# Folding some of the A f products into the A (E - 1) g sums of a graph-attention kernel

## The chip, the cores and the metric

The kernel runs on one core of a Trainium2 chip. The metric is the device time of one execution in microseconds. The engines are named as the profile names them: PE (matrix multiply; PEld is its weight load), DVE (vector), ACT (scalar), POOL and SP, which here mostly issue DMAs.

## The reference

Layer 0 is graph attention over 4096 nodes with a dense 0/1 adjacency A, 8 heads of 64 features; layer 1 is attention inside 32 graphs of 128 nodes. Each is followed by a residual and a layer norm.

```python
feats = jnp.einsum('nf,hfo->hno', X, W)
s_self = jnp.einsum('hno,ho->hn', feats, a_self)
s_neigh = jnp.einsum('hno,ho->hn', feats, a_neigh)
dense = s_self[:, :, None] + s_neigh[:, None, :]
dense = jnp.where(dense > 0, dense, ALPHA * dense)
dense = dense * A[None, :, :]
attn = jax.nn.softmax(dense, axis=-1)
out = jnp.einsum('hij,hjo->hio', attn, feats) + b[:, None, :]
...
a = jnp.where(mask, query @ key.T * scale, 0.0)
scores = (a + b + edge_encoding) * jnp.where(mask, 1.0, -1000000.0)
softmax = jax.nn.softmax(scores, axis=-1) * mask
return softmax @ value
```

Pairs without an edge have the score 0, and so the weight exp(0) = 1. The numerator of layer 0 is therefore the sum of all features, plus the sum over edges of (E - 1) f, where E is the exponential of the score. E is a product of a row factor, a column factor and the larger of two terms, p of the row and d of the column; that is how it is made from two vectors without an exponential for each pair. In the code g is f scaled by its column factor, and u is the row factor that the sum A f still lacks.

## The kernel before

After a setup that makes the features and the exponentials, four passes (`main_pass`, r = 0 to 3) treat two heads each. A pass goes through four chunks c of C = 1024 rows, and a chunk through NT = 32 steps j of 128 neighbours. For a step:

- DVE makes q[j, h] = max(p_row, d_j) * A for both heads (L1475, 128x1024);
- a mark per pair of q is made for the denominators, on ACT (L1485), except for the second head of every fourth step (j % 4 == 3), which DVE makes (L1480);
- PE adds -A f in four matmuls of 128x128 weights to the PSUM tile `accf` (L1499), and A E g in eight matmuls of 32 columns to the tile `acc` (L1521), four of which run beside each other in the array;
- PE adds marks to `dens` (L1536), for eight steps at a time.

At the end of a chunk, `sums_to_rows` makes y = (accf + S) * u + acc on DVE (L1259, L1267), and its pieces, run later, turn y by PE (L1339), divide it (L1340 into `hst`) and send it to memory, or in the last pass hand it to layer 1.

PE's instructions are in the order of the program. Those of the other engines are ordered by a scheduler when the kernel is built, and each engine then works through its queue in that order.

Passes 0 to 2 take groups of eight steps (`wide=8`): all accf matmuls of the group, then all of acc, then dens. Pass 3 takes groups of four. The q tiles go round in a ring of 8 buffers in the wide passes and 6 in the last; a buffer is free when the acc matmuls of its step are done. In pass 0 the adjacency is turned by PE and cast by ACT (L610, L621) and written out; the later passes read it back (`bring`).

In pass 3, from chunk 1 on, `run_plan` puts pieces of layer 1 between the groups by the table PLAN: `pieces(c, group, 0)` between accf and acc, `pieces(c, group, 1)` after dens. "E" is the end of the chunk before; "a" and "b" are the two blocks of 512 rows of that chunk, nine pieces each (`layer_1`: L1075 turns x1, L1095 makes z, L1122 the scores, L1167 the values, L1181 the output); "F" ends a layer norm and "R" starts the second block. `rows_of_layer_0` adds the residual and takes the statistics (L1246, L512). Small PSUM tiles (`misc`, ps_m) go round three banks from pass 1 on. `load_block` and `check_block` stream the adjacency once more to see that it holds only 0 and 1, two ACT operations a block (L1230, L1231).

```python
PLAN = [("E", "b"), ("b", "Fb"), ("b", "a"), ("Ra", "a"), ("Fa", "b"), ("ba", "b")]
PLANS = PLAN + [("ab", ""), ("aaba", "")], PLAN + [("a", ""), ("aa", "a")]
```

Of the kernel before, what the change touches and what calls it, by code (L numbers as in the profile page):

```python
# [10 lines left out]
F32 = mybir.dt.float32  # L11
# [8 lines left out]
P = 128  # L20
# [384 lines left out]
def adjacency_streamed_path(  # L405
# [57 lines left out]
    f_d = dram.tile([PR, NT // 4, P, 4 * 2 * FP], F32, name="f_d")  # L463
    pu_d = dram.tile([2 * H, N], F32, name="pu_d")
    at_d = dram.tile([NCH, NT, P, C], F32, name="at_d")
# [28 lines left out]
    n0 = const.tile([P, NT], F32, name="n0")  # L494
    nb_all = const.tile([P, NT, H], F32, name="nb_all")
    e_all = early.tile([P, NT, 2, H], F32, name="e_all")
    e_b = const.tile([P, NT, H, 6], BF16, name="e_b")
# [39 lines left out]
    hp_ = ctx.enter_context(tc.tile_pool(name="hout", bufs=1))  # L537
    ckp = ctx.enter_context(tc.tile_pool(name="ck", bufs=2))
    ps0 = ctx.enter_context(tc.tile_pool(name="ps_misc", bufs=1, space=PSUM))
# [92 lines left out]
    with tc.tile_pool(name="setup1", bufs=1, side="right") as one, tc.tile_pool(  # L632
# [97 lines left out]
        def exponentials(k, u, sc):  # L730

            j = 4 * k + u
            if u == 0:
                pu_js[k] = two.tile([P, 4, 2, H], F32, name="pu_j")
# [9 lines left out]
            nc.scalar.activation(pu_js[k][:, u], st[:, 3:5], AF.Exp)  # L744
            nc.scalar.activation(d_all[:, j, :], st[:, 2], AF.Exp)

        def parts_of_exponentials(k):
            blk = slice(4 * k, 4 * k + 4)
            nc.vector.tensor_scalar_mul(
                nb_all[:, blk, :], d_all[:, blk, :], -BIG * (1.0 + 2.0**-23)  # L750
            )
            eb = e_b[:, blk]
            for i in range(2):
# [11 lines left out]
        def rows_of_exponentials(k):  # L765
            pr = pss.tile([2 * H, 4, P], F32, name="ps_set")
            for u in range(4):
                nc.tensor.transpose(
                    pr[:, u, :], pu_js[k][:, u].rearrange("p k h -> p (k h)"), ident
                )  # L770
            if k < NB - 1:
                row = late.tile([2 * H, 4 * P], F32, name="pu_row")
            else:
                row = hp_.tile([P, CT, FP], F32, name="hst")
                row = row.rearrange("p t n -> p (t n)")[: 2 * H, : 4 * P]
            rows[k] = row
# [6 lines left out]
        def columns_of_exponentials(k, pc=None):  # L783
            pc = pss.tile([P, 4, 2 * H], F32, name="ps_set") if pc is None else pc
            for u in range(4):
                nc.tensor.transpose(pc[:, u, :], rows[k][:, ts(u, P)], ident[: 2 * H, : 2 * H])
            nc.vector.tensor_copy(
# [140 lines left out]
    def columns_of_last():  # L928

        columns_of_exponentials(NB - 1, misc([P, 4, 2 * H]))  # L930

    psa = ctx.enter_context(tc.tile_pool(name="ps_acc_f", bufs=1, space=PSUM))
    dens = psa.tile([P, HB], F32, name="dens")
# [135 lines left out]
    def layer_1(blk, x1b, lp, lp1, lp2):  # L1069
# [47 lines left out]
        pq = misc([P, 4, P])  # L1117
        ns = lp1.tile([P, 4, P], F32, name="ns")
        nm = small.tile([P, 4], F32, name="nm_f")
# [130 lines left out]
    def sums_to_rows(r, c, acc, accf, ae, u_row, later_by):  # L1250
# [25 lines left out]
        def pieces():  # L1276
# [127 lines left out]
    def main_pass(r, ae=None, wide=4):  # L1404

        for c in range(NCH):
# [8 lines left out]
            for h in range(2):  # L1415
# [5 lines left out]
                    ),  # L1421
                )
            def pieces(c, group, place):
                if r == PR - 1 and c:
# [21 lines left out]
            for j0 in range(0, NT, wide):  # L1446
# [14 lines left out]
                if at_step == 0:  # L1461
                    cast_steps(0, 6, last_pair)
                follow = [
                    x
# [4 lines left out]
                for j in cycle:  # L1469
                    for h in range(2):  # L1470
                        hh = 2 * r + h
                        q = qs[j, h] = ring("q", qp, 6).tile([P, C], F32, name="q")
                        d_j = d_all[:, j, hh : hh + 1]
                        with following(at_step == 0, ("DVE", 3 if j else 2)):
                            ends_of_setup["Q"] = nc.vector.scalar_tensor_tensor(  # L1475
# [40 lines left out]

                for j in cycle:
                    for s in range(2):
                        for o in range(0, FP, 32):
                            h = o // FH  # L1520
                            nc.tensor.matmul(  # L1521
                                acc[o : o + 32, s, :],
                                g_s[j // 4][:, j % 4, h, o % FH : o % FH + 32],
                                qs[j, h][:, ts(s, HB)],
                                start=(j == 0),
                                stop=(j == NT - 1),
                            )
                if r == 0:
# [118 lines left out]
```

## Time and profile before

| what | us |
|---|---|
| median of three runs (2055.07 to 2056.7) | 2055.48 |
| the profiled execution, its own time | 2057.91 |
| its span, first to last instruction | 2056.1 |
| a chunk of pass 0, from L1259 to L1259 | 106.2 |
| a chunk of pass 1 or 2 | 93 to 106 |
| the chunks 0 to 3 of pass 3 | 104.9, 140.7, 170.5, 163.6 |

The end of chunk c of pass 3 is where L1259 starts, at 1443.5, 1584.3, 1754.7 and 1918.3; pass 0 ends so at 565.4. The granted TensorE clock is 0.994 over the span. In the profile a line of a group has the instruction, its output and inputs, the count, then the busy time of all, the mean of one in ns, and the idle time of the engine before them with what ended it. Matmuls overlap, so their mean is longer than their share of the busy time, and one that waits for its input can still count as busy.

### The profile page before, as it was taken

The numbers are of one execution on the slowest core, as the hardware profiler recorded it, in microseconds if no ns is written. First come the engines' busy times: TensorE is split into PE (matmuls) and PEld (weight loads), VectorE is DVE, ScalarE is ACT, GpSimd is POOL, SyncE is SP. The second block draws the span as 40 slices with busy tenths as digits, with TensorE's granted clock in tenths as the row PEclk, the third lists the DMA queues.
The fourth block names the chain that finished last, engine by engine and source line by source line (L and its number), as shares of the span: only waits on it lengthen the run. The fifth ranks groups of instructions, "written<-read, shape, count | busy, mean of one in ns | idle before, by whom it ended". The sixth has DMA issues, their size and how long they took to land.

```text
span 2056.1 us, 38302 instructions
## 1 busy us (share of the span) xinstructions
PE 2030.4 (99%) x15105; PEld 1051.0 (51%) x15105; DVE 1671.9 (81%) x2125; ACT 1542.2 (75%) x1878; POOL 224.2 (11%) x361
## 2 busy tenths in 40 slices
PE   9999999999999999999999999999999999999997
PEld 7884555555544444444454444544454445545453
DVE  5668888888899998798998999999975984896654
ACT  3349888888879889788898989998885666567420
POOL 1222222222100000000000000000210210210111
PEclk9999999999999999999999999999999999999999
DMA  6999999999999999798999999989974764775211
GB/s 208 245 325 259 287 288 276 291 268 289 271 373 337 354 352 335 257 310 298 319 323 340 316 336 323 326 295 358 323 237 144 250 242 137 225 274 169 73 49 43
DMA packets 207371, 551.31 MB, mean 268 GB/s; under 512 B 24780, under 2 KB 65740, under 8 KB 207180
## 3 DMA queue, kind: packets, MB, share of 16 engines
q1 hardware_dynamic: 142828, 426.31, 59.6%
q0 software_dynamic: 62272, 121.91, 23.2%
q8 instruction: 121, 1.98, 0.4%
q10 hardware_dynamic: 2080, 0.52, 0.1%
q14 instruction: 70, 0.57, 0.1%
HBM read 491.79 MB, written 107.22 MB: 291 GB/s over the span
## 4 chain that ended last, share of the span: by engine, by line
PE 93%; DVE 4%; issue 1%; DMA 1%; SPq 0%; POOL 0%; ACT 0%; POOLq 0%; DVEq 0%
PE acc L1521 41%; PE accf L1499 23%; PE ps_fe L800 5%; PE ps_m L1167 5%; PE dens L1536 5%; PE ps_m L1095 5%; DVE q L1475 3%; PE ps_m L1122 1%; PE ps_m L610 1%; PE ps_m L1181 1%; PE ps_m L1075 1%; PE ps_m L1024 1%; PE ps_m L1339 1%; PE ps_set L720 1%; PE ae L1435 1%
## 5 line engine op out<-in xcount | busy, mean ns | idle before, releaser
L1475 DVE SCALAR_TENSOR_TENSOR q<-p_row,d_all,at 128x1024 f32<-128x1024 f32 x1024 | 1242.0, 1277 | 146.9 <-PE acc L1521 121.1
L1485 ACT ACTIVATE mark<-q,nb_all 128x1024 fp8e4<-128x1024 f32 x896 | 995.5, 1145 | 184.3 <-DVE q L1475 168.6
L1521 PE MATMUL acc<-q,g_s 128*32 128x512 f32 x8192 | 903.4, 593 | 1.1 <-DVE q L1475 0.4
L1521 PEld LDWEIGHTS acc<-q,g_s 128*32 128x32 f32 x8192 | 264.1, 110 | 594.4 <-issue 533.0
L1499 PE MATMUL accf<-at,f_s 128*128 128x512 f32 x2048 | 495.2, 398 | 2.1 <-ACT at L621 2.1
L1499 PEld LDWEIGHTS accf<-at,f_s 128*128 128x128 f32 x2048 | 380.3, 188 | 110.4 <-issue 26.4
L1230 ACT ACTIVATE ck<-ck,neg_half_f 128x1024 f32<-128x1024 f32 x128 | 146.0, 1141 | 25.5 <-DMA ck<-in_adj_dram 25.4
L1231 ACT ACTIVATE ck<-ck,neg_quarter 128x1024 f32<-128x1024 f32 x128 | 146.3, 1143 | 1.7
L1536 PE MATMUL dens<-mark,e_b 128*6 128x512 fp8e4 x2048 | 125.3, 379 | 0.0
L800 PE MATMUL ps_fe<-w_sb_f,xT_f 128*128 128x264 f32 (+1 forms) x512 | 121.1, 393 | 1.9 <-ACT xT_f L723 1.9
L621 ACT CAST at<-ps_m 128x1024 fp32r<-128x1024 fp8e4 x124 | 116.4, 1025 | 4.8 <-PE ps_m L610 4.3
L1167 PE MATMUL ps_m<-wvT,x1T 128*128 128x512 f32 x256 | 114.2, 594 | 0.0
L1095 PE MATMUL ps_m<-x1T,M_sb 128*128 128x512 f32 x256 | 112.9, 594 | 0.0
L800 PEld LDWEIGHTS ps_fe<-w_sb_f,xT_f 128*128 128x128 f32 x512 | 100.1, 199 | 16.4 <-ACT xT_f L723 2.5
L1350 POOL DMA_DIRECT2D hs_d<-hst x12 | 10.7, 896 | 847.8 <-DVE hst L1340 847.8
L1480 DVE TENSOR_SCALAR mark<-q,d_all 128x1024 fp8e4<-128x1024 f32 x128 | 96.3, 752 | 4.7
L622 POOL DMA_DIRECT2D at_d<-at x128 | 69.0, 541 | 272.3 <-ACT at L621 248.1
L1536 PEld LDWEIGHTS <-e_b 128*6 128x6 bf16 x2048 | 54.7, 86 | 77.7 <-issue 34.6
L1095 PEld LDWEIGHTS ps_m<-x1T,M_sb 128*128 128x128 f32 x256 | 48.0, 190 | 59.3 <-issue 58.4
L1167 PEld LDWEIGHTS ps_m<-wvT,x1T 128*128 128x128 f32 x256 | 47.6, 190 | 56.4 <-issue 55.2
L1175 DVE TENSOR_TENSOR v_t<-ps_m,bv_row 128x512 f32<-128x512 f32 x32 | 21.7, 684 | 60.5 <-PE ps_m L1167 60.5
L1102 ACT ACTIVATE zT<-ps_m,zb 128x512 f32<-128x512 f32 x32 | 21.7, 680 | 61.2 <-PE ps_m L1095 61.2
(195 smaller groups left out, 1099.5 us busy)
## 6 DMA issues: line engine op xcount, KB each, us to landing
at<-at_d SPq DMA_DIRECT2D x384, 512.0 KB, 6.3
f_s<-f_d SPq DMA_DIRECT2D x128, 512.0 KB, 7.8
at_d<-at POOLq DMA_DIRECT2D x128, 512.0 KB, 14.8
ck<-in_adj_dram SPq DMA_DIRECT2D x128, 512.0 KB, 5.5
g_s<-g_d SPq DMA_DIRECT2D x128, 256.0 KB, 5.6
f_d<-fst POOLq DMA_DIRECT2D x16, 1024.0 KB, 7.9
a_b<-in_adj_dram POOLq DMA_DIRECT2D x32, 512.0 KB, 17.4
p_row<-pu_d SPq DMA_DIRECT2D x32, 512.0 KB, 6.9
```

The costliest lines, as they stand in the source:

```text
L621: ends_of_setup["ACT"] = nc.scalar.copy(at, both[:, :, k])
L800: nc.tensor.matmul(pf[:, q, :, cols], tile_j(xTs[k][:, c].rearrange("p u n -> p (u n)"), u), w_sb[:, c, 4 * q : 4 * q + 4, cols], start=(c ...
L1095: nc.tensor.matmul(pz, L1["M"][:, f, ts(c, P)], x1T[:, f, :], start=(f == 0), stop=(f == FC - 1),)
L1167: nc.tensor.matmul(pv, x1T[:, f, ts(u, P)], L1["wvT"][:, f, :], start=(f == 0), stop=(f == FC - 1),)
L1230: tc.keep_in_program_order(nc.scalar.activation(ck, ck, AF.Square, bias=neg_half))
L1231: nc.scalar.activation(ck, ck, AF.Abs, bias=neg_quarter, accum_out=binp[:, k : k + 1])
L1475: ends_of_setup["Q"] = nc.vector.scalar_tensor_tensor(q, p_row[h], d_j, ats[r, c, j].bitcast(F32), op0=OP.max, op1=OP.mult)
L1480: nc.vector.tensor_scalar(mark, q, d_j, None, op0=OP.is_gt, saturate=False)
L1485: nc.scalar.activation(mark, q, AF.Sigmoid, bias=nb_all[:, j, hh : hh + 1], scale=BIG, saturate=False,)
L1499: nc.tensor.matmul(accf[:, s, :], f_s[j // 4][:, j % 4, w, :], ats[r, c, j][:, ts(s, HB)], start=(j == 0 and w == 0), stop=(j == NT - 1 an ...
L1521: nc.tensor.matmul(acc[o : o + 32, s, :], g_s[j // 4][:, j % 4, h, o % FH : o % FH + 32], qs[j, h][:, ts(s, HB)], start=(j == 0), stop=(j ...
L1536: nc.tensor.matmul(dens[lo : lo + 6, :], e_b[:, j, 2 * r + h, :], marks[j, h][:, ts(s, HB)], start=(j == 0), stop=(j == NT - 1),)
```

## The change

For some steps, called folded, the four A f matmuls are left out. DVE makes q in two operations instead: max(p_row, d_j) times a row U that holds 1/u, then minus a column c = 1/e, times A. With g as the weights this is (E - 1) f over the row factor u, so the eight matmuls of the step add it to `accf`, not to `acc`, and L1259 multiplies it by u later. The mark is a sigmoid of q against a constant.

Folded are, in pass 3, the steps j % 4 == 2 below 28 of chunks 1 to 3 (seven in each); in pass 0, the steps j % 8 == 6 below 24 (6, 14 and 22; in chunk 0 only 14 and 22).

The rows U are loaded once a chunk: in pass 0 into the two `ck` tiles, in pass 3 into the `hst` tile and a new one of the pool lp1. Room is made for these: `ns` and `pT_f` of layer 1 become the tile `a4`, worked on in place, and pass 3 writes the divided rows over y in place of `hst`. The setup takes reciprocals for c (two a block of 512 rows) and for U (two a block, and 20 in place of 16 rows of pu_d).

```diff
+    FOLDED = (0, PR - 1)
+    HU = 2 * len(FOLDED)
+    pu_d = dram.tile([2 * H + HU, N], F32, name="pu_d")
...
+            for r in FOLDED:
+                nc.vector.reciprocal(
+                    c_all[r][:, blk], e_all[:, blk, 1, 2 * r : 2 * r + 2]
+                )
...
+            for i, r in enumerate(FOLDED):
+                nc.vector.reciprocal(
+                    pu_js[k][:, :, 2 * H + 2 * i : 2 * H + 2 * i + 2],
+                    pu_js[k][:, :, H + 2 * r : H + 2 * r + 2],
+                )
...
-        ns = lp1.tile([P, 4, P], F32, name="ns")
+        ns = a4
...
-        pT = lp1.tile([P, 4, P], F32, name="pT_f")
+        pT = a4
...
-            hst = hp_.tile([P, CT, FP], F32, name="hst")
+            if r == PR - 1:
+                hst = y.rearrange("p (t n) -> p t n", t=CT)
+            else:
+                hst = hp_.tile([P, CT, FP], F32, name="hst")
...
+            def folded(j):
+
+                if r == PR - 1:
+                    return r in FOLDED and c > 0 and j % 4 == 2 and j < NT - 4
+                return r in FOLDED and j % 8 == 6 and (0 if c else 8) < j < NT - 8
+
+            def rows_for_folded():
+
+                for h in range(2):
+                    if r == PR - 1:
+                        pool, shape, name = ((hp_, [P, CT, FP], "hst"), (pools.get("lp1"), [P, C], "U_row"))[h]
+                    else:
+                        pool, shape, name = ckp, [P, CK], "ck"
+                    row = pool.tile(shape, F32, name=name)
+                    U_row.append(row.rearrange("p t n -> p (t n)") if len(shape) == 3 else row)
+                    nc.sync.dma_start(
+                        U_row[h],
+                        broadcast_rows(pu_d[2 * H + 2 * FOLDED.index(r) + h, ts(c, C)], P, C),
+                    )
...
+                        if folded(j):
+                            cn = c_all[r][:, j, h : h + 1]
+                            nc.vector.scalar_tensor_tensor(
+                                q, p_row[h], d_j, U_row[h], op0=OP.max, op1=OP.mult
+                            )
+                            nc.vector.scalar_tensor_tensor(
+                                q, q, cn, ats[r, c, j].bitcast(F32), op0=OP.subtract, op1=OP.mult
+                            )
+                            mark = marks[j, h] = sgp.tile([P, C], FP8, name="mark")
+                            nc.scalar.activation(
+                                mark, q, AF.Sigmoid, bias=below_0, scale=2.0**80, saturate=False
+                            )
+                            continue
...
-                    for w in range(2):
+                    for w in range(0 if folded(j) else 2):
...
+                    dst = accf if folded(j) else acc
...
-                                acc[o : o + 32, s, :],
+                                dst[o : o + 32, s, :],
```

More of the change, by code (lines that the diff above doesn't have):

```diff
@@ L463, in adjacency_streamed_path @@
     f_d = dram.tile([PR, NT // 4, P, 4 * 2 * FP], F32, name="f_d")
-    pu_d = dram.tile([2 * H, N], F32, name="pu_d")
+    FOLDED = (0, PR - 1)
+    HU = 2 * len(FOLDED)
+    pu_d = dram.tile([2 * H + HU, N], F32, name="pu_d")
     at_d = dram.tile([NCH, NT, P, C], F32, name="at_d")
@@ L495, in adjacency_streamed_path @@
     nb_all = const.tile([P, NT, H], F32, name="nb_all")
+    c_all = {
+        r: (const if r else early).tile([P, NT, 2], F32, name="c_all") for r in FOLDED
+    }
+    below_0 = const.tile([P, 1], F32, name="below_0")
+    nc.gpsimd.memset(below_0, -128.0)
     e_all = early.tile([P, NT, 2, H], F32, name="e_all")
@@ L537, in adjacency_streamed_path @@
     hp_ = ctx.enter_context(tc.tile_pool(name="hout", bufs=1))
-    ckp = ctx.enter_context(tc.tile_pool(name="ck", bufs=2))
     ps0 = ctx.enter_context(tc.tile_pool(name="ps_misc", bufs=1, space=PSUM))
@@ L733, in exponentials @@
             if u == 0:
-                pu_js[k] = two.tile([P, 4, 2, H], F32, name="pu_j")
+                pu_js[k] = two.tile([P, 4, 2 * H + HU], F32, name="pu_j")
             st = small.tile([P, 5, H], F32, name="st")
@@ L743, in exponentials @@
             nc.scalar.activation(e_all[:, j], st[:, 0:2], AF.Exp)
-            nc.scalar.activation(pu_js[k][:, u], st[:, 3:5], AF.Exp)
+            nc.scalar.activation(
+                pu_js[k][:, u, : 2 * H].rearrange("p (k h) -> p k h", k=2), st[:, 3:5], AF.Exp
+            )
             nc.scalar.activation(d_all[:, j, :], st[:, 2], AF.Exp)
@@ L765, in rows_of_exponentials @@
         def rows_of_exponentials(k):
-            pr = pss.tile([2 * H, 4, P], F32, name="ps_set")
+            for i, r in enumerate(FOLDED):
[3 more added lines that the diff above has]
+                )
+            pr = pss.tile([2 * H + HU, 4, P], F32, name="ps_set")
             for u in range(4):
-                nc.tensor.transpose(
-                    pr[:, u, :], pu_js[k][:, u].rearrange("p k h -> p (k h)"), ident
-                )
+                nc.tensor.transpose(pr[:, u, :], pu_js[k][:, u], ident)
             if k < NB - 1:
-                row = late.tile([2 * H, 4 * P], F32, name="pu_row")
+                row = late.tile([2 * H + HU, 4 * P], F32, name="pu_row")
             else:
                 row = hp_.tile([P, CT, FP], F32, name="hst")
-                row = row.rearrange("p t n -> p (t n)")[: 2 * H, : 4 * P]
+                row = row.rearrange("p t n -> p (t n)")[: 2 * H + HU, : 4 * P]
             rows[k] = row
@@ L785, in columns_of_exponentials @@
             for u in range(4):
-                nc.tensor.transpose(pc[:, u, :], rows[k][:, ts(u, P)], ident[: 2 * H, : 2 * H])
+                nc.tensor.transpose(
+                    pc[:, u, :], rows[k][: 2 * H, ts(u, P)], ident[: 2 * H, : 2 * H]
+                )
             nc.vector.tensor_copy(
@@ L930, in columns_of_last @@
         columns_of_exponentials(NB - 1, misc([P, 4, 2 * H]))
+    ckp = ctx.enter_context(tc.tile_pool(name="ck", bufs=2))
     psa = ctx.enter_context(tc.tile_pool(name="ps_acc_f", bufs=1, space=PSUM))
@@ L1422, in main_pass @@
                 )
+            U_row = []
+            def folded(j):
[14 more added lines that the diff above has]
+                    )
             def pieces(c, group, place):
@@ L1462, in main_pass @@
                     cast_steps(0, 6, last_pair)
+                if not U_row and any(folded(j) for j in cycle):
+                    rows_for_folded()
                 follow = [
@@ L1473, in main_pass @@
                         d_j = d_all[:, j, hh : hh + 1]
+                        if folded(j):
[5 more added lines that the diff above has]
+                                q, q, cn, ats[r, c, j].bitcast(F32), op0=OP.subtract, op1=OP.mult
+                            )
+                            mark = marks[j, h] = sgp.tile([P, C], FP8, name="mark")
+                            nc.scalar.activation(
+                                mark, q, AF.Sigmoid, bias=below_0, scale=2.0**80, saturate=False
+                            )
+                            continue
                         with following(at_step == 0, ("DVE", 3 if j else 2)):
@@ L1526, in main_pass @@
                                 stop=(j == NT - 1),
+                                skip_group_check=folded(j),
                             )
```

## The prediction, made before the changed kernel ran

> **What bounds the kernel now.** I read the page's busy times first, then its costliest groups, then the table by stretches, then the timelines of PE and DVE inside one group of steps. The page and its groups:
>
> ```profile
> PE 2030.4 (99%) x15105; PEld 1051.0 (51%) x15105; DVE 1671.9 (81%) x2125; ACT 1542.2 (75%) x1878; POOL 224.2 (11%) x361
> ...
> L1475 DVE SCALAR_TENSOR_TENSOR q<-p_row,d_all,at 128x1024 f32<-128x1024 f32 x1024 | 1242.0, 1277 | 146.9 <-PE acc L1521 121.1
> ...
> L1521 PE MATMUL acc<-q,g_s 128*32 128x512 f32 x8192 | 903.4, 593 | 1.1 <-DVE q L1475 0.4
> ...
> L1499 PE MATMUL accf<-at,f_s 128*128 128x512 f32 x2048 | 495.2, 398 | 2.1 <-ACT at L621 2.1
> ```
>
> PE is the longest queue, and DVE is second at 81%, all its idle time spent waiting for PE to give q buffers back. That average hides two different stages. By stretches (start:end, length, then busy time of each engine; the first lies in the first pass, the second and third are the first and the second half of chunk 1 of the last pass):
>
> ```profile
> 248.00:353.00 105.00, 104.66 (x966) 52.83 (x959) 87.12 (x91) 91.58 (x90) 25.78 (x41) 1.00 1.11 285
> ...
> 1444.00:1503.00 59.00, 58.57 (x472) 27.24 (x468) 58.77 (x82) 49.77 (x70) 14.29 (x8) 1.00 0.95 322
> 1503.00:1584.00 81.00, 81.00 (x445) 40.84 (x438) 46.73 (x63) 55.91 (x77) 5.89 (x10) 1.00 0.51 167
> ```
>
> The third number is DVE: 87 of 105 in the first pass, but 58.8 of 59 where the changed steps of chunk 1 begin. Now one group of eight steps of the first pass, DVE and then PE (start, length, instruction, count, idle before):
>
> ```profile
> 381.52 10.85 DVE L1475 SCALAR_TENSOR_TENSOR q<-p_row,d_all,at 128x1024 f32<-128x1024 f32 x9 [3.80 <-PE acc L1521]
> 392.30 0.74 DVE L1480 TENSOR_SCALAR mark<-q,d_all 128x1024 fp8e4<-128x1024 f32 x1
> ```
>
> ```profile
> 378.50 1.07 PE L610 MATMUL ps_m<-ident_b,a_b 128*128 128x128 bf16 x16
> 379.49 13.94 PE L1521 MATMUL acc<-q,g_s 128*32 128x512 f32 x128
> 393.37 0.66 PE L1282 MATMUL ps_m<-ident_f,hst 128*128 128x128 f32 x4
> ```
>
> PE takes (393.37-379.49)/8 = 1.735 us for a step of acc. DVE sits full at eight q tiles (four steps), starts the fifth step's q 2.03 us after acc began, when the first step's buffers are free, and makes one q each (10.85-1.28)/8 = 1.196 us, 2.39 us for a step. The eighth q ends at 381.52+7x1.196+1.28 = 391.17; PE wants it at 379.49+7x1.735 = 391.63. So DVE, idle 3.8 us before the group, catches the last step by 0.46 us. The last pass, chunk 1, PE:
>
> ```profile
> 1450.82 3.93 PE L1499 MATMUL accf<-at,f_s 128*128 128x512 f32 x16
> 1454.59 0.60 PE L1316 MATMUL ps_m<-ident_f,dcs 128*128 128x128 f32 x4
> ...
> 1455.99 7.52 PE L1521 MATMUL acc<-q,g_s 128*32 128x512 f32 x64
> ...
> 1467.31 9.44 PE L1521 MATMUL acc<-q,g_s 128*32 128x512 f32 x62
> ...
> 1482.69 7.07 PE L1521 MATMUL acc<-q,g_s 128*32 128x512 f32 x64
> ...
> 1495.25 7.07 PE L1521 MATMUL acc<-q,g_s 128*32 128x512 f32 x64
> ```
>
> An undisturbed acc of four steps is 7.07; those of 7.52 and 9.44 waited for q inside, though PE counts as busy. DVE is what ends here. The accf group gives (1454.59-1450.82)/16 = 0.236 us a matmul.
>
> **What the Trainium skill says.** "Perfetto Trace Analysis", Identifying the Most-Contended Engine, says that busy share of matmuls misleads because they are pipelined, and its Optimization Strategy says that the contended engine can change between regimes; both hold here (the acc of 9.44 us). "TensorE: Matmul & The Clock Gate", Part 3, says that matmuls run as a strict FIFO in start and end: one late q holds all behind it. "VectorE: DVE Perf Modes", the perf-mode tier table, gives two-tensor fp32 work only the 1x rate (2293 ns for 2048 elements, so an estimate of 1.15 us for 1024); the trace has 1.196 from start to start. So no cheaper form of the added operation is to be hoped for.
>
> **The change part by part.** Folded steps: last pass 7 in each of chunks 1 to 3, 21; first pass 2 in chunk 0 and 3 in each other, 11; in all 32.
>
> Removed: 4 accf matmuls a step, 4x0.236 = 0.94 us, 32x0.94 = 30.1 us of PE. The eight matmuls of E only change their bank: 0.
>
> Added: two DVE operations a step. The second reads q, a column and the adjacency, the form of L1475, so 2x1.196 = 2.39 us a step, 76.5 us in all. They are issued h0, h1, h0, h1, so the dependent one finds its input ready. The mark stays on ACT with the same shape (1145 ns): 0.
>
> First pass. The folded step is the seventh of eight, so its extra 2.39 falls where DVE is catching up. The last q comes at 391.17+2.39 = 393.56, PE is there at 391.63: 1.93 late. From such a late q to PE's next group the trace of chunk 2 of the last pass has 1.90 us (q ends 1616.70, next 1618.60), 0.17 over a step, so 2.10. Against it 0.94 from accf: +1.16 a group. DVE's idle 3.8 before the next acc covers its own lateness, so nothing carries over. 11 x 1.16 = **+12.8**. Both ends: the wait can't fall under 1.93-0.94 = 1.0 a group, nor pass 2.39+0.17-0.94 = 1.6: +11 to +18.
>
> Last pass, chunk 1. Here the fold is the third of four steps and six q are made ahead, but DVE has no idle time to make them in. Until the fourth group's last q, DVE gets 4x2.39 = 9.6 more, and the built program's queue order puts about 3.0 us of layer-norm work (an hp_l add of 0.5; five x1b adds and two stats, 1495.03 to 1497.50) behind that q: 1499.97+9.6-3.0 = 1506.6, acc ends 1.9 later at 1508.5 against 1502.14. PE's accf savings up to there are eaten by this wait. Walking queue by queue gives 5.9. From group 4 on PE has layer-1 matmuls and DVE idles (46.7 of 81), so three folds save 0.94 each: +5.9-2.8 = **+3.1**.
>
> Chunks 2 and 3 have the same start, with less DVE load at group 0 (-0.2 there). In group 1 the queue order puts the second evacuation of the turned sums (L1340, 1621.62 before) behind the layer-norm statistics, at about 1626.1. The three banks ps_m go round, so the second values matmul (1622.57 before) waits for that bank, its v_t and the q behind it come later: +4.3 by the end of group 1. Group 2 -0.5, group 3 +3.8 (DVE bound again), groups 4 to 6 -2.8: **+4.7** each, +9.4. Both ends for the last pass: if DVE's lateness were absorbed, -0.94x21 = -19.7; if each added operation landed whole, 21x(2.39-0.94) = +30.5.
>
> Other edits. Two hp_l adds go out of chunk 0, where DVE is busy 96 of 104: -0.9. At the end of setup two reciprocals come ahead of the last row transposes, and a cast that accf waits for (L621, 156.73) goes behind the row copy: +1.0; 0 to +1.5. The other reciprocals (some 30, under 0.25 us each by L1332's row) fall in DVE's idle setup time: 0. Fourteen row loads of 512 KB (6.9 us as p_row's) are queued on SP one group ahead: 0; if SP were held behind their DVE wait, the at loads (6.3 us) behind them would be late, at most a few us for each of 3 chunks. The in-place a4, and y for hst: a buffer's reuse that the plan leaves free for groups: 0, up to +2 in the tail.
>
> Sum: 12.8 + 3.1 + 9.4 - 0.9 + 1.0 = +25.4. The profiled execution took 2057.9 with a span of 2056.1, so its span would be 2081.5; the median of the runs, 2055.48, becomes **2081**, +1.2%.
>
> **The rivals.** (a) The last pass absorbs it: DVE idles 3 to 10 us at a time in the second half of each chunk, and if late q are made up there PE keeps its 19.7: 2055.5+12.8+1.0-19.7 = 2050, faster. It decides if the acc of groups 0 to 3 grow by less in all than 0.94 a fold, some 20 us over three chunks. Against it: PE's lost time is not returned, as PE is itself full afterwards. (b) All is hidden: DVE at 81% has room on average: 2055.5-30 = 2025; against it the 0.46 us of room above. (c) Each added operation lands whole: 2055.5+76.5-30.1 = 2102; for it, DVE's 58.8 of 59 and bank waits like that of group 1 elsewhere; against it, groups 4 to 6. (d) The first pass as computed, the last one about even: 2055.5+13.8 = 2069, on the forecast's side.
>
> **How the numbers follow.** Forecast with its size errors, 2072 to 2094: 0.66; (d) 0.12; (c) 0.11; (a) 0.08; (b) 0.03. The range 2064 to 2096 takes (d), the forecast and the lower edge of (c). A measurement here tells about 0.2% (4 us) from no change. Faster: (a)+(b) with a bit less, 0.10; same 0.02; slower 0.88.
>
> **What would show it.** Right: in the first pass the acc runs of folded groups last about 16.0 in place of 13.94, and those of the fourth group of each chunk stay; accf groups of 28 matmuls; chunks of 109.7 in place of 106.2. In the last pass, acc runs of groups 0 to 3 well over 7.07, those of 4 to 6 at 7.07; DVE idle only in the second halves; chunk 1 longer by 3, chunks 2 and 3 by 5. Wrong: first-pass acc runs still of 13.94 (the ring ran further ahead than I read), or last-pass chunks shorter by 6.6, which is (a).

## The result, and the profile after

| | before | after |
|---|---|---|
| median of six runs each, us | 2055.28 (2051.77 to 2056.70) | 2080.06 (2076.24 to 2086.44) |
| ratio after/before, 95% interval | | 1.0125 [1.0108, 1.0143] |
| the profiled execution, its span, us | 2056.1 | 2080.0 |

The change costs 24.8 us, within 1 us of the forecast. The page of the changed kernel, engines and then the groups that the change touches (the numbers behind the bar: busy us, mean ns of one | idle before it, released by):

```profile
PE 2035.5 (98%) x14977; PEld 1027.0 (49%) x14977; DVE 1747.2 (84%) x2221; ACT 1535.9 (74%) x1876; POOL 235.4 (11%) x362
...
L1533 DVE SCALAR_TENSOR_TENSOR q<-p_row,d_all,at 128x1024 f32<-128x1024 f32 x960 | 1166.6, 1277 | 114.4 <-PE acc L1580 103.7
...
L1580 PE MATMUL acc<-q,g_s 128*32 128x512 f32 x7680 | 872.2, 594 | 4.4 <-DVE q L1533 1.8
...
L1557 PE MATMUL accf<-at,f_s 128*128 128x512 f32 x1920 | 468.3, 399 | 1.7 <-ACT at L627 1.6
...
L1580 PE MATMUL accf<-q,g_s 128*32 128x512 f32 x512 | 80.8, 611 | 12.3 <-DVE q L1524 9.6
L1524 DVE SCALAR_TENSOR_TENSOR q<-q,c_all,at 128x1024 f32<-128x1024 f32 x64 | 79.2, 1276 | 0.0
```

The kernel does what it says: 128 accf matmuls fewer than the 2048 of before, and 64 second operations (L1524), each as long as an L1533. PE has less to do and its busy time still rises by 5 us. The rise is the first pass's (with the folds of that pass alone PE is busy 2040.3, with those of the last pass alone 2022.7). There a folded step starts when the first head's q is there, two matmuls at a time in place of four (395.26 and 395.72 in the group shown below), and goes on when the second head's q is: that stretch counts as busy. Only the row of folded products (accf<-q) shows some of the wait in the open, 12.3 us idle. Its mean of 611 against 594 ns comes mostly from 16 matmuls of chunk 1 of the last pass that ran at half clock, of which more below.

The same stretches as before, shifted to where the chunks now lie (start:end, length, then PE, PEld, DVE, ACT and POOL; behind them PE's clock, DMA share and GB/s):

```profile
252.00:357.00 105.00, 104.03 (x926) 48.48 (x919) 93.62 (x96) 86.24 (x86) 25.39 (x41) 1.00 1.11 290
1455.00:1520.00 65.00, 58.71 (x477) 25.24 (x468) 65.00 (x81) 50.98 (x70) 28.79 (x6) 0.95 0.91 304
1520.00:1599.00 79.00, 78.86 (x419) 38.43 (x416) 57.78 (x80) 54.23 (x68) 6.76 (x9) 1.00 0.57 187
```

In the first half of chunk 1 of the last pass DVE is busy 65.00 of 65, and that half grew from 59 to 65. PE's granted clock there is 0.95, where it was 1.00 before. The second half shrank from 81 to 79, with DVE still idle for 21 us of it. So the loss lies in the first halves, and in the first pass.

For all kernels of this study I use one measure: the time from the start of one chunk's first operation of y (L1259 before, L1277 after) to that of the next, from the trace. Differences from before, us; "first" is the span's start to the first y, setup and chunk 0 together, "end" what follows the last y:

| kernel | first | pass 0, chunks 1, 2, 3 | pass 3, chunk 0 | chunks 1, 2, 3 | end |
|---|---|---|---|---|---|
| after | +2.5 | +3.36, +3.31, +3.39 | -1.6 | +3.90, +4.75, +3.39 | +0.8 |
| first pass only | +4.5 | +3.36, +3.30, +3.38 | -1.2 | +0.03, 0.00, +0.34 | -1.2 |
| last pass only | -2.3 | +0.05, -0.02, +0.03 | -0.1 | +4.19, +3.69, +2.67 | -1.6 |
| third of eight | -3.1 | -2.35, +2.43, -0.09 | +0.6 | +3.50, +3.05, +3.06 | -1.5 |
| two operations, accf kept | +5.7 | +5.83, +5.75, +5.80 | +0.5 | +0.04, -0.01, +0.39 | -1.6 |
| one operation, rows loaded | +14.7 | -2.35, -2.47, -2.38 | +0.1 | +0.05, +0.02, 0.00 | -1.3 |
| one operation, no rows | +0.1 | -2.35, -2.46, -2.38 | -1.7 | +0.03, 0.00, +0.02 | -1.6 |
| evacuations first | +1.3 | +3.37, +3.29, +3.39 | -0.8 | +3.33, +3.09, +3.04 | +1.6 |
| early half, one operation | -2.1 | +0.06, -0.02, +0.03 | -0.4 | -1.44, -1.55, -2.99 | +0.6 |
| late nine | -0.4 | +0.06, -0.04, +0.03 | +0.4 | -2.69, -2.71, -2.68 | +0.1 |
| late five a chunk | -0.1 | +0.06, -0.02, +0.03 | -1.0 | -4.52, -4.56, -4.56 | 0.0 |
| late eight a chunk | +1.5 | +0.05, -0.03, +0.02 | -0.6 | 0.00, -0.91, -1.83 | -3.8 |
| late eight and third | -1.6 | -2.38, +1.10, +1.95 | -0.2 | +0.01, -0.86, -1.74 | -3.2 |

Passes 1 and 2 never differ by more than 0.5 in a chunk. The columns "first", "chunk 0" and "end" scatter by 2 to 3 us between kernels that differ nowhere near them: the kernels without folds in the first pass have -2.3 to +1.5 in "first". PE's clock seems to have a part in it: its mean over that stretch is 0.99 in last pass only (-2.3), 0.98 before and 0.97 in late eight (+1.5). The other six columns repeat to a tenth where the code there is the same, except that in the last pass a chunk with the same folds differs by up to 1.7 us from kernel to kernel (chunk 2: +4.75 in after, +3.05 in third of eight). In the two late-eight rows the first operation of y at the end of chunk 1 stands behind other work in DVE's queue: PE starts the last acc group of that chunk 1.9 us sooner after the chunk's beginning than before, and 1.9 us of their "end" belongs to the chunks. The execution of before that the table is taken from took 2057.9, which is 2 to 3.5 us above the medians of before in the experiments: by about so much the medians show more loss, or less gain, than the chunks.

**The first pass, seen.** One folded group of eight, PE, then DVE (start, length, count, idle before):

```profile
376.91 6.97 PE L1557 MATMUL accf<-at,f_s 128*128 128x512 f32 x28
...
384.72 10.51 PE L1580 MATMUL acc<-q,g_s 128*32 128x512 f32 x96
395.26 2.68 PE L1580 MATMUL accf<-q,g_s 128*32 128x512 f32 x14
...
398.11 2.65 PE L1580 MATMUL acc<-q,g_s 128*32 128x512 f32 x14
400.69 0.66 PE L1300 MATMUL ps_m<-ident_f,hst 128*128 128x128 f32 x4
```

```profile
386.75 4.87 DVE L1533 SCALAR_TENSOR_TENSOR q<-p_row,d_all,at 128x1024 f32<-128x1024 f32 x4 [3.17 <-PE acc L1580]
391.54 2.48 DVE L1521 SCALAR_TENSOR_TENSOR q<-p_row,d_all,ck 128x1024 f32<-128x1024 f32 x2
393.93 2.48 DVE L1524 SCALAR_TENSOR_TENSOR q<-q,c_all,at 128x1024 f32<-128x1024 f32 x2
396.32 3.67 DVE L1533 SCALAR_TENSOR_TENSOR q<-p_row,d_all,at 128x1024 f32<-128x1024 f32 x3
```

From 384.72 to 400.69 the group takes 15.97; before it took 393.37-379.49 = 13.88. The first six steps (96 matmuls) run at full pace. DVE gets its first free buffer 2.03 us after acc began, as before, makes four q and the two folded ones, and ends the second L1524 at 396.41; until then PE has only the first head's half of the seventh step. The seventh and eighth step then follow DVE, not PE. DVE still has 3.17 us idle before the group, so the next group starts clean.

**The last pass, seen.** Chunk 1, group 1, PE:

```profile
1476.83 3.64 PE L1580 MATMUL acc<-q,g_s 128*32 128x512 f32 x32
1485.02 1.92 PE L1580 MATMUL accf<-q,g_s 128*32 128x512 f32 x4 [4.56 <-DVE q L1524]
1488.68 2.77 PE L1580 MATMUL accf<-q,g_s 128*32 128x512 f32 x10 [1.73 <-DVE q L1524]
...
1492.83 0.60 PE L1596 MATMUL dens<-mark,e_b 128*6 128x512 fp8e4 x4
```

This acc took 16.0 us from its start to dens; an undisturbed one takes 7. DVE in that time (it has no gap there):

```profile
1478.01 1.19 DVE L1521 SCALAR_TENSOR_TENSOR q<-p_row,d_all,hst 128x1024 f32<-128x1024 f32 x1
1479.12 1.28 DVE L1361 TENSOR_TENSOR ys<-ps_m,rd 128x512 f32<-128x512 f32 x2
...
1481.13 1.27 DVE L519 BATCH_NORM_STATS2 stats_f<-x1b 128x6 f32<-128x512 f32 x2
...
1483.72 1.25 DVE L1524 SCALAR_TENSOR_TENSOR q<-q,c_all,at 128x1024 f32<-128x1024 f32 x1
...
1487.35 1.27 DVE L1524 SCALAR_TENSOR_TENSOR q<-q,c_all,at 128x1024 f32<-128x1024 f32 x1
```

The end of the chunk before and its statistics stand between the two operations of the fold. After the wait of 4.56 us PE's granted clock was halved for about 6.8 us, from 1485.0 on (the length, PE's busy time, then the clock):

```profile
1485.00:1492.00 7.00, 5.25 (x24) 0.51 1.07 372
```

Matmuls that start 0.43 us apart in other groups start 0.83 apart here. From the end of the last q (1488.54+1.27) to the end of the acc run, about 1493.7, it takes 3.9 us, where the group of the first pass above took 1.9; so 2 us is an estimate of what the halving cost in this group.

In chunk 2 the long one is group 3. PE (the last line is where the acc of group 4 begins), then DVE, then POOL there:

```profile
1681.69 1.92 PE L1580 MATMUL acc<-q,g_s 128*32 128x512 f32 x16
1684.54 3.11 PE L1580 MATMUL acc<-q,g_s 128*32 128x512 f32 x16 [0.93 <-DVE q L1533]
1689.33 2.68 PE L1580 MATMUL accf<-q,g_s 128*32 128x512 f32 x14 [1.68 <-DVE q L1524]
...
1713.17 3.64 PE L1580 MATMUL acc<-q,g_s 128*32 128x512 f32 x32
```

```profile
1682.30 1.00 DVE L527 TENSOR_SCALAR y_f<-y_f,mv_f,rstd_f 128x512 f32<-128x512 f32 x2 [3.05 <-POOL rstd_f L523]
```

```profile
1680.67 0.19 POOL L1130 TENSOR_SCALAR off<-off 128x4 f32<-128x4 f32 x1 [20.06 <-ACT a L1123]
...
1681.54 0.72 POOL L523 TENSOR_TENSOR rstd_f<-rstd_f,neg_half 128x2 f32<-128x2 f32 x1
```

Here DVE is wanted most, and stands idle for 3.05 us: its next instruction in order scales by rstd_f, and on POOL rstd_f is queued behind `off`, which waited 20 us for ACT. Six q of the group, two of them folded, are queued on DVE behind that wait, and PE behind them. (The Trainium skill, "Perfetto Trace Analysis", Tensor Engine Instruction (MATMUL, LD_WEIGHTS), says that ACT, DVE and GpSimd work in strict order; here rstd_f, which needs only mv_f, indeed starts after `off`.) Before, the acc runs of groups 3 and 4 of chunk 2 began like this, and the same scaling waited 0.62 us:

```profile
1665.22 7.14 PE L1521 MATMUL acc<-q,g_s 128*32 128x512 f32 x62
...
1692.05 7.07 PE L1521 MATMUL acc<-q,g_s 128*32 128x512 f32 x64
```

```profile
1659.71 1.00 DVE L520 TENSOR_SCALAR y_f<-y_f,mv_f,rstd_f 128x512 f32<-128x512 f32 x2 [0.62 <-POOL rstd_f L516]
```

The wait goes further back. ACT's L1123, for which `off` waited, itself waited for the load of the adjacency block `a`, which SP issued late:

```profile
1679.31 0.31 ACT L1123 ACTIVATE a<-a 128x128 f32<-128x128 f32 x1 [5.34 <-DMA a<-in_adj_dram]
```

```profile
1671.77 0.38 SPq L1098 DMA_DIRECT2D a<-in_adj_dram  x1
```

This is the tile a4. Before, ACT waited for such a load once in the last pass, 0.91 us; after, five times, 2.25 to 5.34 us. The change keeps a4 in use for longer, as the home of pT_f: PE last reads it in L1199, here until 1668.6, where before it was free after L1131. That this is why the load is late is likely, but no run takes the in-place a4 out alone. It takes POOL's order too: in the late-nine run below, which has the in-place a4, ACT waits 7.77 us for the load in chunk 2, but there rstd_f stands ahead of `off`, and DVE waits 0.62. PE's wait of 1.29 us for ACT just before this group (at 1681.11, for x1T) has the same source, since that copy stands behind L1123.

### The profile page after: what moved, and what is told of

It reads as the page before. It is cut to its first block, busy times and chain, and to the rows that moved or that the text cites. A ratio compares the mean times of both kernels' runs of the same rounds, so it can differ in the third digit from the quotient of the medians.

```text
span 2080.0 us, 38133 instructions
## 1 busy us (share of the span) xinstructions
PE 2035.5 (98%) x14977; PEld 1027.0 (49%) x14977; DVE 1747.2 (84%) x2221; ACT 1535.9 (74%) x1876; POOL 235.4 (11%) x362
## 4 chain that ended last, share of the span: by engine, by line
PE 85%; DVE 9%; issue 2%; DMA 2%; ACT 1%; POOL 0%; SPq 0%; DVEq 0%; POOLq 0%; ACTq 0%
PE acc L1580 34%; PE accf L1557 21%; PE ps_fe L817 5%; PE dens L1596 5%; PE ps_m L1185 5%; PE ps_m L1113 5%; DVE q L1533 4%; DVE q L1521 2%; PE ps_m L616 1%; PE ps_m L1140 1%; PE ps_m L1199 1%; PE accf L1580 1%; DVE q L1524 1%; PE ae L1478 1%; PE ps_m L1042 1%
## 5 line engine op out<-in xcount | busy, mean ns | idle before, releaser
L1533 DVE SCALAR_TENSOR_TENSOR q<-p_row,d_all,at 128x1024 f32<-128x1024 f32 x960 | 1166.6, 1277 | 114.4 <-PE acc L1580 103.7
L1543 ACT ACTIVATE mark<-q,nb_all 128x1024 fp8e4<-128x1024 f32 x832 | 921.0, 1147 | 170.9 <-DVE q L1533 159.3
L1580 PE MATMUL acc<-q,g_s 128*32 128x512 f32 x7680 | 872.2, 594 | 4.4 <-DVE q L1533 1.8
L1580 PEld LDWEIGHTS acc<-q,g_s 128*32 128x32 f32 x7680 | 246.7, 110 | 569.7 <-issue 486.6
L1557 PE MATMUL accf<-at,f_s 128*128 128x512 f32 x1920 | 468.3, 399 | 1.7 <-ACT at L627 1.6
L1557 PEld LDWEIGHTS accf<-at,f_s 128*128 128x128 f32 x1920 | 356.7, 189 | 106.7 <-issue 28.5
L1528 ACT ACTIVATE mark<-q,below 128x1024 fp8e4<-128x1024 f32 x64 | 72.6, 1146 | 41.7 <-DVE q L1524 40.6
L1580 PE MATMUL accf<-q,g_s 128*32 128x512 f32 x512 | 80.8, 611 | 12.3 <-DVE q L1524 9.6
L1524 DVE SCALAR_TENSOR_TENSOR q<-q,c_all,at 128x1024 f32<-128x1024 f32 x64 | 79.2, 1276 | 0.0
```

Of the source, the lines that this page charges most:

```text
L1524: nc.vector.scalar_tensor_tensor(q, q, cn, ats[r, c, j].bitcast(F32), op0=OP.subtract, op1=OP.mult)
L1533: ends_of_setup["Q"] = nc.vector.scalar_tensor_tensor(q, p_row[h], d_j, ats[r, c, j].bitcast(F32), op0=OP.max, op1=OP.mult)
L1543: nc.scalar.activation(mark, q, AF.Sigmoid, bias=nb_all[:, j, hh : hh + 1], scale=BIG, saturate=False,)
L1557: nc.tensor.matmul(accf[:, s, :], f_s[j // 4][:, j % 4, w, :], ats[r, c, j][:, ts(s, HB)], start=(j == 0 and w == 0), stop=(j == NT - 1 an ...
L1580: nc.tensor.matmul(dst[o : o + 32, s, :], g_s[j // 4][:, j % 4, h, o % FH : o % FH + 32], qs[j, h][:, ts(s, HB)], start=(j == 0), stop=(j ...
```

## The experiments

Each is after.py with the edit shown; a ratio is to runs of the kernel before on the same chip.

**First pass alone.** The last pass folds nothing.

```diff
                 if r == PR - 1:
-                    return r in FOLDED and c > 0 and j % 4 == 2 and j < NT - 4
+                    return False
```

> Only the eleven folded steps of the first pass are kept; every other edit stays. Theory (a folded step costs where DVE's extra 2.39 us makes q late at its place in the group): first pass as in the changed kernel, three chunks of 109.6 us and +12.6 in all, last pass within 2 us of before; about 2068 us. Rival A (the side edits cost: row loads on SP, the reused tiles, the queue order they bring): the last pass stays about 11 us longer without its folds, about 2079. Rival B (DVE's total load costs, wherever it stands): 22 of 64 operations, so about a third of 25: 2064.

2071.31, ratio 1.0086 [1.0070, 1.0103]; the profiled execution has a span of 2068.7. The chunks of the first pass repeat those of after, the last pass is as before.

**Last pass alone.** The first pass folds nothing.

```diff
-                return r in FOLDED and j % 8 == 6 and (0 if c else 8) < j < NT - 8
+                return False
```

> Only the 21 folded steps of the last pass are kept. Theory: chunks of the first pass back at 106.2 us, the last pass +11 as in the changed kernel: about 2066.5 us. Rival A: the first pass keeps part of its 12.6. Rival B: two thirds of 25, so 2072.

2070.99 (2064.73 to 2073.19), ratio 1.0087 [1.0070, 1.0104]; the profiled span is 2062.9, from the lowest of its four runs. Chunks 1 to 3 lose 10.6 in all; after, they lose 12.0. By the chunks the two parts make up nearly what the whole loses (10.0+10.6 against 10.1+12.0). The medians do not add up: the two runs lie 17.0 and 16.6 us above before, the whole 24.8. Part of that is the execution of before (see under the table), part the scatter of the setup; the rest stays open.

**The fold in the third step of eight.** Same number of folds in the first pass, four steps earlier; last pass as after.

```diff
-                return r in FOLDED and j % 8 == 6 and (0 if c else 8) < j < NT - 8
+                return r in FOLDED and j % 8 == 2 and (8 if c == 0 else 0) <= j < NT - 8
```

> The eleven folded steps of the first pass are moved from the seventh to the third of their group of eight (same count, same operations), the last pass as in the changed kernel. Theory: the extra 2.39 us then falls into q that DVE makes ahead, in its 3 to 5 us of idle time, so acc runs of folded groups go back to about 13.9 us and each group gains 0.94: first pass -10.3 instead of +12.6, total about 2056 us. Rival B: the place doesn't matter, 2080. Rival A: no change from 2080 either, since every load and tile is as before.

2065.29, ratio 1.0053 [1.0034, 1.0073]. A folded acc run, chunk 1, PE:

```profile
295.69 3.64 PE L1580 MATMUL acc<-q,g_s 128*32 128x512 f32 x32
...
309.56 0.65 PE L1334 MATMUL ps_m<-ident_f,dcs 128*128 128x128 f32 x4
```

It takes 309.56-295.69 = 13.87, as an unfolded one. So it is the place in the group that made the q late, not the added work. But the gain was had in one chunk only (-2.35). At the start of chunk 2, and of chunk 3 with 2.08, PE now waits for something new:

```profile
365.57 7.03 PE L1557 MATMUL accf<-at,f_s 128*128 128x512 f32 x28
375.62 1.07 PE L616 MATMUL ps_m<-ident_b,a_b 128*128 128x128 bf16 x16 [3.02 <-DMA a_b<-in_adj_dram]
```

The adjacency loads of this stretch (247 to 562 us) took a median of 21.2 us from issue to landing, before 17.8. PE was 3 us too early for one. The wait is not all that it costs in chunk 2: PE's granted clock was then halved for about 3.4 us (the clock is the third number from the end):

```profile
376.60:380.20 3.60, 3.60 (x22) 1.03 (x24) 0.00 (x0) 3.34 (x4) 0.86 (x3) 0.53 1.03 408
```

At half speed 1.7 us of work are lost there; with the 3.02 that makes 4.7, and 2.43+2.35 is 4.8. After the wait of 2.08 the clock stayed at 1.00.

**Two operations, accf kept; and one operation, accf left out.** Both in the first pass alone. In the first A f is counted once too often in the folded steps, in the second it is missing there.

```diff
-                    for w in range(0 if folded(j) else 2):
+                    for w in range(2):
```

> First pass alone, 11 folded steps, with the second DVE operation added but the four accf matmuls of each folded step kept, so that A f is counted once too often there. Theory (the folded step's last q comes 2.1 us late and nothing hides it): 11 x 2.1 = +23 us, near 2078; the acc run of a folded group stays near 16.0, its accf group is back at 32 matmuls; 7 to 10 us above the run that folds in the first pass alone. Rival (the lateness was caused by the shorter accf group itself, which brings PE to acc 0.94 earlier): acc runs near 15.0, no more than +13 us, near 2068.

2080.09, ratio 1.0112 [1.0093, 1.0131]. The folded group of eight in chunk 2:

```profile
382.54 7.60 PE L1557 MATMUL accf<-at,f_s 128*128 128x512 f32 x32
...
390.98 10.51 PE L1580 MATMUL acc<-q,g_s 128*32 128x512 f32 x96
...
406.95 0.66 PE L1300 MATMUL ps_m<-ident_f,hst 128*128 128x128 f32 x4
```

From 390.98 to 406.95 it takes 15.97, to the hundredth that of after, with all 32 accf matmuls in place. The chunks are longer by 5.8 in place of 3.35. So the second operation costs 5.8/3 = 1.93 us a fold in the first pass, and the accf matmuls are worth (5.79-3.35)/3 = 0.81.

```diff
                             nc.vector.scalar_tensor_tensor(
-                                q, p_row[h], d_j, U_row[h], op0=OP.max, op1=OP.mult
-                            )
-                            nc.vector.scalar_tensor_tensor(
-                                q, q, cn, ats[r, c, j].bitcast(F32), op0=OP.subtract, op1=OP.mult
+                                q, p_row[h], d_j, ats[r, c, j].bitcast(F32), op0=OP.max, op1=OP.mult
                             )
```

> First pass alone, the 11 steps keep one DVE operation and lose their four accf matmuls, so that A f is left out there. Theory: acc runs back at 13.9, and 11 x 0.94 = -10.3 us, near 2044. Rival (the adjacency loads of the first pass are its second floor, as the run with the fold in the third step of eight showed): part of it comes back as waits of PE for the adjacency load at the start of a group, -2 to -7 us, near 2050.

2065.8, ratio 1.0044 [1.0029, 1.0059]: a kernel with less work for PE than before and no more in DVE's steps, and slower. The chunks 1 to 3 give 2.4 each (0.80 a fold), but setup and chunk 0 lose 14.7. PE at that place (L1554 is L1557 in this kernel), SP's queue, and what SP's row loads (L1461) waited for in that stretch (us in total, times, longest):

```profile
205.34 4.95 PE L1554 MATMUL accf<-at,f_s 128*128 128x512 f32 x12 [12.55 <-DMA f_s<-f_d]
```

```profile
183.75 10.56 SPq L1461 DMA_DIRECT2D ck<-pu_d  x4
...
194.83 0.42 SPq L1495 DMA_DIRECT2D f_s<-f_d  x1
...
SPq L1461 <- DMA ck<-pu_d: 20.3, 6, 6.1
```

Since no operation reads the two rows any more, nothing holds their loads back: all eight, for four chunks, go out in chunk 0, two buffers for all, each waiting for the load before it in its buffer to land. The f_s load at 194.83 stands behind that line on SP. PE's wait for f_s is 12.55 of the 14.7; behind it the clock stayed at half until about 209.5, and the twelve accf matmuls took 4.95 us where twelve of them take 3.0 elsewhere. Neither the theory nor the rival had this.

**The same without the rows.** So the loads were taken out too.

```diff
-                if not U_row and any(folded(j) for j in cycle):
-                    rows_for_folded()
```

> As the first-pass run with one DVE operation (accf matmuls and second operation left out in the 11 steps, so A f is missing there), but the two rows that nothing reads are not loaded. Theory (the 14.7 us that the earlier run lost in chunk 0 came from SP, held in a line of row loads that waited for one another's landing, so that f_s was issued late): no such wait, chunks 1 to 3 of the first pass shorter by 2.4 each, near 2047. Rival (the first pass has no room because of its DMA traffic itself): chunk 0 or a later one again longer, 2055 or more.

2049.13, ratio 0.9970 [0.9959, 0.9981]. The 14.7 us are gone, the chunks gain as before. It also bounds what the third-of-eight run showed: its chunks are as short as the shortest there (103.8), and PE waits for no adjacency load. Short chunks alone do not make it late; that run also loads rows (1 MB a chunk) and has other orders on POOL, which issues the adjacency loads. Which of these it is was not tried.

**Evacuations first.** After, with the layer-norm rows of the last pass given out behind both evacuations of the turned sums (L1361).

```diff
-                if t4 == 0:
+                if t4 == 4:
                     if r == PR - 1:
                         first = rows_of_layer_0(2 * c, hst, pools["lp"])
```

> The changed kernel with one reorder: the layer-norm rows of the last pass are given out behind both evacuations of the turned sums rather than between them. Theory of the prediction (the second evacuation is held behind the statistics, and v_t and the q behind it come late): chunks 2 and 3 shorter by about 3 us each, near 2074. Rival (DVE's queue in group 1 is full anyway, and the order within it moves nothing): within 1.5 us a chunk, 2078 to 2082.

2079.97, ratio 1.0121 [1.0103, 1.0139], as after. Chunk 2 gained 1.66 and chunk 3 0.35, but not by this order: by the end of the acc run of group 1 they had gained 0.2 and 0.6, and the run with the third of eight, whose last pass is that of after, has the same chunks to 0.2 us. So the order in group 1 is worth 0.6 us at most, and perhaps nothing.

**The early half with one operation.** Last pass, groups 0 to 3 of chunks 1 to 3, twelve steps without their accf matmuls (A f is missing there), one operation as before.

```diff
-                    return r in FOLDED and c > 0 and j % 4 == 2 and j < NT - 4
-                return r in FOLDED and j % 8 == 6 and (0 if c else 8) < j < NT - 8
+                    return r in FOLDED and c > 0 and j % 4 == 2 and j < NT // 2
+                return False
```

with the two edits of the first-pass runs above (one operation, rows not loaded).

> Last pass only, the folded steps of groups 0 to 3 of chunks 1 to 3 (12 in all), with one DVE operation as before and their accf matmuls left out, so that A f is missing there. Theory (in these groups DVE sets the end, so what PE saves there is eaten by its wait for q): 0 to -1.5 us for each chunk, near 2053. Rival (PE sets the end there and keeps its saving): 4 x 0.94 = -3.8 for each chunk, near 2044.

2052.42, ratio 0.9989 [0.9981, 0.9998]. Of 3.76 us that PE saves in a chunk, 1.4 and 1.6 are kept in chunks 1 and 2, 3.0 in chunk 3. Chunk 1, group 1, where PE comes 1.02 us early and waits for q (line numbers are 5 lower here; L1528 is L1533):

```profile
1464.58 5.07 PE L1575 MATMUL acc<-q,g_s 128*32 128x512 f32 x30 [1.02 <-DVE q L1528]
```

Late q thus took more than half of the saving in chunks 1 and 2 before any operation was added; in chunk 3 they mostly did not, and the theory is too strong there.

**Late folds.** Only groups 4 to 6 of chunks 1 to 3 of the last pass: one step in each (nine), then five steps a chunk, then eight.

```diff
-                    return r in FOLDED and c > 0 and j % 4 == 2 and j < NT - 4
-                return r in FOLDED and j % 8 == 6 and (0 if c else 8) < j < NT - 8
+                    return r in FOLDED and c > 0 and j % 4 == 2 and NT // 2 <= j < NT - 4
+                return False
...
+                    return r in FOLDED and c > 0 and j in (18, 22, 24, 25, 26)
...
+                    return r in FOLDED and c > 0 and j in (18, 19, 22, 23, 24, 25, 26, 27)
```

> No fold in the first pass; in the last pass only the folds of groups 4, 5 and 6 (three in each of chunks 1 to 3, nine in all). Theory: there DVE idles 3 to 10 us at a time, so each fold gains 0.94 us, 8.5 in all: about 2047 us (2044 to 2049). Rival A: the last pass stays about 11 longer, 2066. Rival B: nine times 2.39-0.94, so 2068.

2049.72, ratio 0.9977 [0.9970, 0.9983]: 0.90 a fold, faster than both kernels.

> No folds in the first pass; in the last pass five in each of chunks 1 to 3, all in its groups 4 to 6, where DVE idles. Theory (a fold where DVE idles is pure gain of 0.94): 15 x 0.94 = -14 us, near 2040, and chunks 1 to 3 shorter by 4.7 each. Rival (three folds in one group of four use up DVE's idle time there, and its last q are late): no better than nine late folds, 2046 to 2050, with acc runs over 7.07 in group 6.

2045.52, ratio 0.9954 [0.9938, 0.9971], the fastest of the study: by the chunks again 0.9 a fold. Group 6 has its first three steps folded and runs as an undisturbed one (7.01 from its start to the next):

```profile
1565.86 5.36 PE L1580 MATMUL accf<-q,g_s 128*32 128x512 f32 x48
1571.04 1.90 PE L1580 MATMUL acc<-q,g_s 128*32 128x512 f32 x16
1572.87 3.94 PE L1557 MATMUL accf<-at,f_s 128*128 128x512 f32 x16
```

> No folds in the first pass; in the last pass eight in each of chunks 1 to 3, two, two and four in groups 4, 5 and 6. Theory (DVE idles some 34 us in that half of a chunk, and eight folds take 19): 24 x 0.9 = -21.6, near 2034, and each chunk shorter by 7.2. Rival (four folds in group 6 overrun DVE there): chunks shorter by less than the 4.5 of five folds, 2042 or more, with the acc run of group 6 over 7.07.

2052.77, ratio 0.9985 [0.9979, 0.9992]: three more folds a chunk give back most of the gain. Group 4, from its third step on:

```profile
1524.30 1.90 PE L1580 MATMUL accf<-q,g_s 128*32 128x512 f32 x16
1526.61 3.11 PE L1580 MATMUL accf<-q,g_s 128*32 128x512 f32 x16 [0.40 <-DVE q L1524]
1529.64 1.09 PE L1093 MATMUL ps_m<-ident_f,x1b 128*128 128x128 f32 x8
```

The last step starts 0.6 late and takes 3.03, undisturbed 1.83: the group lasts 8.79 in place of 7.0 and returns the 1.8 by which PE came to it earlier. Neither side had quite this: it is not only group 6, with four folds, but each group whose last two steps are folded. DVE had idle time on average (34 us in the half before), and 3.43 us of it right before the folded q of this group, waiting for a buffer; it had none in the few us between the buffers coming free and the last step.

**Late eight and the third of eight.** Both edits together.

> The eight late folds of each of chunks 1 to 3 of the last pass, and in the first pass one step in eight, the third. Theory (the first pass gains about 2.4 in one chunk and gives as much back in waits for the adjacency load): 0 to -4 us against the run with eight late folds alone, near 2032. Rival (both gains add without a second floor): 11 x 0.9 = -10 more, near 2024.

2050.1, ratio 0.9975 [0.9965, 0.9985]; 2.7 under late eight alone, the first pass giving -2.38, +1.10 and +1.95. The gain of one chunk is again given back in the next two, so the first pass is left unfolded in the best version.

## Why the prediction was right, point by point

**The sum.** +25.4 was forecast, the spans differ by 23.9. First pass without chunk 0, nine folds: 9 x 1.16 = +10.4 forecast, +10.1 measured. Last pass: +12.5 forecast for chunks 1 to 3, +12.0 measured.

**The first pass** was right in its mechanism and nearly in its terms. Forecast: acc runs of about 16.0, measured 15.97; 2.10 late, measured 2.09; accf groups of 28. That DVE's idle time before the next acc covers its lateness holds (3.17 us left). The term for accf was 0.94 a fold, and 0.81 was measured; the second operation's own effect on a chunk was 1.93 a fold. Both are smaller by about the same, so the difference of 1.12 came out.

**Last pass, second halves.** Forecast were -2.8 a chunk, and the late folds alone measure -2.7. In the kernel itself groups 4 to 6 save less, 1.2 in chunk 1 and 2.2 in chunks 2 and 3: the acc run of group 4 was to last 7.07 and took 8.18, 7.39 and 7.43, still waiting for q. Take the -2.7 off and the first halves with that tail lost 6.6, 7.5 and 6.1; forecast were 5.9, 7.4 and 7.4.

**The steps that failed** are in chunks 2 and 3, and in each other's favour. What these chunks had lost, by the ends of the acc runs and from the chunk's own start:

| by the end of the acc run of | forecast | chunk 2 | chunk 3 |
|---|---|---|---|
| group 1 | +4.3 | +1.5 | +1.6 |
| group 2 | +3.8 | +0.9 | +1.1 |
| group 3 | +7.6 | +7.0 | +5.6 |
| the whole chunk | +4.7 | +4.75 | +3.39 |

First, "+4.3 by the end of group 1", the bank held by the second evacuation: the wait exists (in chunk 2 PE waits 1.06 for L1361, then 0.67), but the loss is 1.5, and putting the evacuations first got back 0.6 at most.

Second, a term put at nothing, "the in-place a4 [...] a buffer's reuse that the plan leaves free for groups: 0". Group 3 was given +3.8, all of it DVE's own work, and lost 6.1 in chunk 2 and 4.5 in chunk 3. In the trace DVE also waits for rstd_f there, at the end of the line that begins with the late load of a4 and goes through `off` on POOL. Four kernels have these folds, and the wait differs among them (what is lost from the end of the acc run of group 2 to that of group 3, then the wait, us):

| | after | last pass only | third of eight | evacuations first |
|---|---|---|---|---|
| chunk 2 | 6.07, 3.05 | 5.40, 2.39 | 4.57, 1.53 | 4.85, 1.83 |
| chunk 3 | 4.51, 1.49 | 4.52, 1.48 | 4.52, 1.48 | 4.23, 1.20 |

The loss less the wait is 3.01 to 3.04 in all eight: each microsecond of the wait is lost whole. PE also starts the group late, but waits for q inside it all the same (0.93 and 1.68 us in chunk 2), so DVE's line is the one that comes last. As 0.6 us of the wait was there before, DVE's own work comes to 3.6, with 3.8 forecast. That the wait lengthens the group is shown by these eight cases; that the reuse of a4, with POOL's new order, causes the wait is read from the trace and not tested alone. Two wrong sizes made up a right sum for these chunks, which is luck.

**Chunk 1**, +3.1 forecast and +3.9 measured. By the end of group 3 it had lost 5.1, forecast 5.9; that it ends higher all the same is group 4's wait. The loss comes in group 1 (+5.6 by its end), 16.0 us of acc, where the folds of two groups meet the statistics on DVE and where PE then ran at half clock, some 2 us, which the prediction did not have.

**A reading.** DVE's idle time before was not all a wait for PE to give q back: that is 121 of some 384 us. The first pass and the first halves, on which the sum rests, are not touched by it.

**Small terms.** Chunk 0 of the last pass, -0.9, the setup, +1.0, and the end, 0, lie within the scatter of those columns, and were neither shown nor refuted. The risk that SP is held behind a row load was put at nothing for the kernel as it is, and it does not show there; the run with unread rows shows what it costs if it comes true, 14.7 us.

**The rivals.** (a), the last pass absorbs it, is refuted by the last pass alone: its three chunks are longer by 10.6, where (a) had them shorter by 19.7. (d), the last pass about even, is refuted by the same run. (c), each operation whole, fits the first halves of the chunks and no other place: there four folds cost 6.1 to 7.5, and 4 x (2.39-0.94) is 5.8; but the half clock in chunk 1 and the wait for rstd_f in chunks 2 and 3 are part of that cost, so the operations alone cost less. (b) has its place too: the late folds are hidden. The kernel's result is a mean over places with opposite signs, and a version with the late folds alone has only the good ones.

## What to carry to other kernels

Work moved to an engine that is idle on average is free only where that engine is ahead when its result is wanted: look at the last buffer of each group, not at the busy share. Fold the early steps of a group, and only in stretches where the other engine really waits; past the point where its slack in one group ends, each further step gives back what it saved. When a stage gets faster, look for the load that will be late next, and when a tile is reused to make room, for what the tile's next load feeds.

## What was not expected of the hardware

- A kernel with less work for PE was slower: row loads that nothing reads, in a line on SP, held f_s back and cost 14.7 us (12.55 of it one wait of PE). In the changed kernel the same eight loads go out between 168 and 449 us, each only when the rows before it have been read; without readers all went out between 170 and 194.
- A wait of PE can cost more than its length. After waits of 3.02, 4.56 and 12.55 us PE's granted clock was 0.50 for 3.4 to 6.8 us (in the last case also during the wait). It is not so each time: after one of 3.42 us, in the run with late eight and third, the clock stayed at 1.00, after one of 2.56 it was halved. No rule is worked out here.
- The wait of a late operand shows little as idle time. In the late-eight run an idle 0.40 stands beside a step that took 3.03 in place of 1.83: its first matmuls run two at a time in place of four (at 1526.61 and 1527.06), as the second head's q is not there yet, and that counts as busy. The section of the Trainium skill named above also says that the end of a matmul is computed from its size, not observed; the distance of starts is the safer reading here.
